# Sums in one piece, and the attention's first tiles beside the feed-forward's last steps, in a two-layer macaron block

## The chip, the core and the metric

The kernel runs on one core of a Trainium2 chip. It is written engine by engine: TensorE (PE) multiplies matrices and writes to PSUM, VectorE (DVE) and ScalarE (ACT) work on SBUF and PSUM, GpSimd (POOL) on SBUF, and SyncE (SP) issues transfers. Each engine takes its own instructions in order, and semaphores tie them together. The metric is the device time of one execution in microseconds; what counts is the median of several runs.

## The reference

One sequence of 2048 positions with 256 features passes two macaron layers. Every sub-block normalises its input first (LayerNorm), and its result is added to the residual.

```python
x = x + 0.5 * ffn0(layernorm(x))      # f0: ternary weights, silu(gate) * up, rms norm, projection
x = x + attn0(layernorm(x))           # 16 heads of 16, ALiBi bias, causal softmax
x = x + 0.5 * ffn0(layernorm(x))      # f1
x = x + 0.5 * ffn1(layernorm(x))      # f2: silu(gate) * up, 2 of 4 kept by magnitude, projection
x = x + attn1(layernorm(x))           # biases, rotary embedding (RoPE), causal softmax
x = x + 0.5 * ffn1(layernorm(x))      # f3

# attention, per head
scores = q @ k.T / 4 (+ alibi) ; scores = where(j > i, -inf, scores)
y = softmax(scores) @ v ; out = concat(y) @ W_o
```

## The kernel before

**Layout.** Features lie on partitions, positions run along the free axis. The 2048 positions are four chunks of 512 (`c`, NCH = 4); x and its normalised copy are one tile per chunk (`xs`, `xns`).

**Order.** The engines' instruction order is the order in which the Python code records them (`manual_schedule` for PE, ACT, DVE and POOL); only SP's transfers are put in order by the framework. Work that is to lie beside other work is a generator: each `next()` records one more piece, up to its `yield`. Such generators are the quantiser of the ternary weights, LayerNorm (`pieces`, in `background`), `sparsify`, the tail of a feed-forward, and the attention's preparation.

**Feed-forward.** `feed_forwards` goes through chunks and, in each, through eight steps f. A step is one gate-and-up product (`pg_f`), SiLU on ACT, a product on DVE. Steps of f0 and f1 work on three-part bf16 splits (12 matmuls); those of f2 and f3 are fp32, and every fourth one starts `sparsify` (`ge_f`, `ct_f`, `h_f` on DVE and POOL). The projection of a chunk (`po_f`) and its update of x lie in the next chunk's steps; the last chunk's come after all steps. In f0 the row sums of squares `ss_f` (POOL) go to the product `pss_f` before the projection. After every step, `beside` may record something of the attention that follows.

**Attention.** `attention` is a generator with two parts. The first yield hands out `first()`, whose pieces `beside0` and `beside1` record one per feed-forward step; `attend()` records what is left of it and then the whole rest. `prep_qk(c, "k")` and `prep_qk(c, "q")` multiply a chunk by the weights (`pp_k`, `pp_q`), split the result into three bf16 parts (ACT, DVE, POOL: `p_k`, `p_q`) and have SP write them to DRAM in six transfers (`dk<-p_k`, `dq<-p_q`). In layer 1 the rotary step comes before: two SP transfers swap halves (`sw`), POOL and DVE multiply by cosines and sines, DVE adds; the tiles `dn` and `sw` have one buffer there, and the generator has five pieces instead of two. `prep_v` makes v with a column of ones (`va`). `load(n, kc)` reads the four heads of group n (16 groups, four per chunk) back from DRAM, stacked so that one matmul over 96 rows gives the score of a head to fp32 accuracy, and adds rows for biases and maxima.

**Slots.** The rest runs over slots: a slot is a group n and a block `kb` of 128 keys (4, 8, 12 or 16 slots per group). For each slot:

- `st_pair`: keys by queries, two heads at a time, into a PSUM pair (`pst`); two pairs exist.
- `exp_pair`: the exponential on ACT, 128x1024 (`pT`).
- `mx_unit`: a tile of queries by keys of a later group (`pq`, one of three single PSUM banks), reduced to row maxima on DVE (`mx`). `mx_end` joins a group's maxima and splits them (`neg`); one step later `mx_turn` turns them with four small matmuls (`ptm`), ACT copies them (`qx`) and three transfers put them into the rows 96 to 98 of the group's q, so that the exponential's argument has its maximum subtracted.
- `av_part`: the sums `pav` of four heads, each in its own 32 columns of the array, over one half of the queries (part 0, part 1). On the diagonal, after part 0, `divide` transposes the 128 finished columns on DVE (`yt`), takes reciprocals (`rd`) and POOL multiplies (`zt`). Later `turn_back` and `output` finish a chunk (`pwo`).

On the diagonal a slot covers 512, 384, 256, then 128 queries; part 1 exists only if more than 256 are covered. A table `maxima` says which tiles go into which slot; slot -1 stands for the seven tiles that are needed before slot 0 (four of group 0, three of group 1). 140 of the 160 slots have tiles, all but the last ones.

In a slot with tiles the sums stand in two places: behind the first pair of heads the second half of the unit two slots back, behind the second pair the first half of the previous unit. Without tiles both halves of the previous unit stand together:

```python
for hp in (1, 0):
    ps = st_pair(n, kb, hp)
    mx_next(units[0], (2 - 2 * hp, 3 - 2 * hp))
    pTs[hp] = exp_pair(n, kb, hp, ps)
    sums(i - 2 + (hp == 0), hp)
```

The tiles of q, k and of the maxima are allocated in pools `kv` and `at` that open when the feed-forward's pool has closed; chunk 1's k, q and v are prepared between the seven tiles of slot -1. `need` records the pieces of a preparation until it is done.

Of the kernel before, what the change touches and what calls it, by code (L numbers as in the profile page):

```python
# [26 lines left out]
G = 4  # L27
# [19 lines left out]
def macaron_kernel(ctx: ExitStack, tc: tile.TileContext, a, out):  # L47
# [37 lines left out]
        )  # L85


    ident = cpool.tile([P, P], F32, name="ident")
    make_identity(nc, ident)
    ident_b = cpool.tile([P, P], BF16, name="ident_b")  # L90
    nc.vector.tensor_copy(ident_b, ident)

    mask_qk = cpool.tile([P, P], BF16, name="mask_qk")
    mask_kq = cpool.tile([P, P], BF16, name="mask_kq")
# [395 lines left out]
    def attention(layer, following):  # L490
# [9 lines left out]
        with ExitStack() as st:  # L500
# [20 lines left out]
            def prep_qk(c, what):  # L521

                ready(c)
                if what == "k" and c > 0:
                    nc.gpsimd.memset(va[c], 1.0)
                at = 0 if what == "q" else DC
                name = f"{layer}_{what}{c}"
                dn = ka.tile([P, DC, CH], F32, tag="dn", bufs=2 - layer, name=f"dn{name}")
                pt = [
                    ka.tile([P, DC, CH], BF16, tag=f"part{j}", bufs=1, name=f"p{j}{name}")  # L530
                    for j in range(3)
                ]
                for i in range(DC):
                    pp = ps_one(f"pp{name}_{i}")
                    for dc in range(DC):
                        nc.tensor.matmul(  # L536
                            pp,
                            lhsT=wqkv[:, dc, (at + i) * P : (at + i + 1) * P],
                            rhs=xns[c][:, dc, :],
                            start=dc == 0,  # L540
                            stop=dc == DC - 1,
                        )
                    if layer == 0:
                        nc.scalar.copy(pt[0][:, i, :], pp)
                        nc.vector.tensor_tensor(dn[:, i, :], pp, pt[0][:, i, :], ALU.subtract)
                    else:
                        nc.scalar.activation(
                            dn[:, i, :], pp, AF.Identity, bias=b_qk[:, at + i : at + i + 1]
                        )
                    if i == 0:  # L550
                        yield
                if layer == 1:

                    sw = ka.tile([P, DC, CH], F32, tag="sw", bufs=1, name=f"sw_{what}{c}")
                    for o in range(2):
                        nc.sync.dma_start(
                            out=sw[o * 64 : o * 64 + 64, :, :],
                            in_=dn[64 - o * 64 : 128 - o * 64, :, :],
                        )
# [14 lines left out]
                    for i in range(DC):  # L574
                        nc.gpsimd.tensor_tensor(sw[:, i, :], sw[:, i, :], cs[:, 1, :], ALU.mult)
                    yield
                    nc.vector.tensor_tensor(dn, dn, sw, ALU.add)
                    nc.scalar.copy(pt[0], dn)
                    nc.vector.tensor_tensor(dn, dn, pt[0], ALU.subtract)
                nc.scalar.copy(pt[1], dn)  # L580
                nc.gpsimd.tensor_tensor(pt[2], dn, pt[1], ALU.subtract)
                for j in range(3):
                    for m, part in enumerate(Q_PARTS if what == "q" else K_PARTS):
                        if part == j:
                            nc.sync.dma_start(
                                out=parts[what, c][:, m, :, :].rearrange("i p t -> p i t"),
                                in_=pt[j],
                            )
                done.add((what, c))
                yield  # L590
# [24 lines left out]
                        done.add(("v", c))  # L615
                    yield

            def first():
                nc.gpsimd.memset(va[0], 1.0)
                yield  # L620
                for work in (prep_qk(0, "k"), prep_qk(0, "q"), prep_v(0)):
                    yield from work

            yield first()
            kv = st.enter_context(tc.tile_pool(name=f"kv{layer}", bufs=1))
            ap = st.enter_context(tc.tile_pool(name=f"at{layer}", bufs=2))
            va += [values(kv, c) for c in range(1, NCH)]
            acc = ps_acc(f"pav{layer}")
            zts = {}
            zs = {}  # L630


            qs = {}
            ks = {}

            def load(n, kc):
                c, g = divmod(n, G)

                def stack(to, what, of, extra):
                    nc.sync.dma_start(  # L640
                        out=to[0:RM],
                        in_=parts[what, of][g // 2]
                        .rearrange("m (d u) t -> (m d) u t", u=HB)[:, g % 2 * 4 : g % 2 * 4 + 4, :],
                    )
# [12 lines left out]


# [40 lines left out]
            def mx_turn(n):  # L699
# [3 lines left out]
                for t in range(T):  # L703
# [4 lines left out]
                        start=True,  # L708
                        stop=True,
                    )  # L710
                qx = ap.tile([12, CH], BF16, tag="qx", bufs=2, name=f"qx{layer}_{n}")
                nc.scalar.copy(qx, pt)
                for m in range(3):
                    nc.sync.dma_start(out=qs[n][RM + m : RM + m + 1, :, :], in_=qx[4 * m : 4 * m + 4, :])
                turned_max.add(n)


            def banks(name, apart):
# [161 lines left out]
            def need(*what):  # L880
                while what not in done:
                    assert preps, what
                    step()

            left = {}
            for units in maxima.values():
                for u in units:
# [17 lines left out]

            def load_to(slot):
                while uses and uses[0][1] <= slot:
                    load(*uses.popleft()[0])
# [30 lines left out]
            for i, (n, kb) in enumerate(slots):  # L939
# [72 lines left out]

    def begin(layer, following):
        att = attention(layer, following)
        begun[:] = att, next(att)

    def beside0(s, at, f):
        if not quants and not begun:
            raw_scope.close()
            begin(0, "f1")  # L1020
        if at == NCH - 1:
            next(begun[1], None)

    def beside1(s, at, f):
        if s == 1 and at == 0 and f == FC // 2:
            own.close()
            ffn0_scope.close()
            begin(1, "f3")
        if s == 1 and (at == NCH - 1 or at == NCH - 2 and f >= FC // 2):
            next(begun[1], None)  # L1030
# [134 lines left out]
```

## Time and profile before

| | us |
|---|---|
| median of three runs | 1954.04 (1952.93 to 1957.03) |
| profiled execution, its own time | 1957.69 |
| its span | 1955.7 |
| PE busy | 1761.4 |
| DVE busy | 1361.6 |
| ACT busy | 894.2 |
| POOL busy | 458.4 |
| mean granted PE clock | 0.96 |

The profile shows one execution. A row of a timeline gives start, duration, engine, line, operation, output and inputs with shapes, a count, and in brackets how long the engine was idle before and what ended that. Durations of matmuls include the pipeline's depth, so what one occupies is read from the difference of two starts. Attention of layer 0 runs from about 240 to 766 us, that of layer 1 from about 1175 to 1766 us; the feed-forward f0 ends at 231, f1 and f2 fill about 766 to 1169, f3 the rest.

### The profile page before, as it was taken

Reading aid. Unit: us, or ns where it says so; the run is one execution under the profiler, and the core shown is the slowest. Engines: PE = TensorE matmul, PEld = TensorE weight load, DVE = VectorE, ACT = ScalarE, POOL = GpSimd, SP = SyncE. Lnnn points to the kernel's source line nnn. Section 1 sums busy time; section 2 is a strip of 40 time slices with the busy share of each in tenths; the row PEclk is TensorE's granted clock in tenths of the full one; section 3 lists DMA queues with packets and bytes.
Section 4 is the critical chain, followed back from the end, with each engine's and each line's share of the span. In section 5 each row is a group of like instructions: output and inputs, shape, how many; then the busy total and the mean of one; then the engine's idle time right before and its main releaser. Section 6 shows DMA issues by size and latency. Waiting matters only on the chain. (4 is left out here: it accounts for less than half of the span.)

```text
span 1955.7 us, 26994 instructions
## 1 busy us (share of the span) xinstructions
PE 1761.4 (90%) x10684; PEld 726.5 (37%) x10684; DVE 1361.6 (70%) x2384; ACT 894.2 (46%) x1112; POOL 458.4 (23%) x418
## 2 busy tenths in 40 slices
PE   5699789999999999789999876898999999998997
PEld 1233344433433333333444333433333333333443
DVE  7866377787788883666575655868877888825664
ACT  4343254555555668334422312445555656673220
POOL 3455321101000000455453432211111000003422
PEclk9799899999999999989999986999999999999999
DMA  4000252213211000200000115222122110000000
GB/s 129 1 1 33 82 148 83 73 54 102 62 45 46 28 28 2 73 1 0 1 11 0 54 61 158 82 73 92 52 69 86 43 43 26 18 1 0 11 11 22
DMA packets 50510, 93.10 MB, mean 48 GB/s; under 512 B 5424, under 2 KB 33072, under 8 KB 50128
## 3 DMA queue, kind: packets, MB, share of 16 engines
q1 hardware_dynamic: 49296, 89.28, 14.8%
q10 hardware_dynamic: 1088, 2.10, 0.3%
q8 instruction: 84, 1.38, 0.3%
q14 instruction: 42, 0.34, 0.1%
HBM read 59.51 MB, written 27.26 MB: 44 GB/s over the span
## 5 line engine op out<-in xcount | busy, mean ns | idle before, releaser
L682 DVE TENSOR_REDUCE mx<-pq 128x1 f32<-128x512 f32 (+3 forms) x1280 | 708.6, 603 | 158.5 <-PE pq L679 91.2
L753 ACT ACTIVATE pT<-pst 128x1024 f32<-128x1024 f32 (+3 forms) x614 | 542.6, 896 | 334.9 <-PE pst L733 196.8
L671 PE MATMUL pq<-k,q 105*128 105x512 bf16 (+7 forms) x1280 | 378.8, 353 | 74.7 <-DVE mx L682 52.3
L733 PE MATMUL pst<-q,k 99*128 99x512 bf16 (+7 forms) x1280 | 357.7, 354 | 5.1 <-ACT pT L753 4.2
L768 PE MATMUL pav<-pT,va 128*32 128x256 f32 (+1 forms) x4608 | 352.4, 382 | 5.2 <-DVE yt L789 5.0
L281 PE MATMUL pg_f<-xn,wgu 128*128 128x512 f32 x512 | 229.8, 602 | 11.5 <-DVE hr_f L318 11.5
L794 POOL TENSOR_TENSOR zt<-yt,rd 128x64 f32<-128x64 f32 x128 | 38.4, 300 | 795.2 <-DVE rd L793 795.1
L733 PEld LDWEIGHTS <-k 105*128 105x128 bf16 (+1 forms) x1280 | 101.5, 98 | 254.1 <-issue 218.4
L317 ACT ACTIVATE sl_f<-pg_f 128x512 f32<-128x512 f32 x128 | 76.0, 594 | 251.8 <-PE pg_f L281 175.0
L671 PEld LDWEIGHTS <-q 105*128 105x128 bf16 (+1 forms) x1280 | 124.5, 100 | 148.0 <-issue 44.3
L306 PE MATMUL pg_f<-xn,wgu 128*128 128x512 bf16 x512 | 156.2, 413 | 19.5 <-DVE wgu L170 6.8
L768 PEld LDWEIGHTS pav<-pT,va 128*32 128x32 f32 x4608 | 93.8, 108 | 208.7 <-issue 174.8
L281 PEld LDWEIGHTS pg_f<-xn,wgu 128*128 128x128 f32 x512 | 98.6, 193 | 136.9 <-issue 121.0
L306 PEld LDWEIGHTS <-wgu 128*128 128x128 bf16 x768 | 77.7, 101 | 166.9 <-issue 74.7
L292 PE MATMUL po_f<-h_f,wd 128*128 128x512 f32 x256 | 116.3, 608 | 17.3 <-DVE h_f L418 17.3
L340 POOL TENSOR_TENSOR ss_f<-ss_f,sq_f 128x512 f32<-128x512 f32 x56 | 91.1, 1628 | 111.5 <-ACT sq_f L339 111.3
L679 PE MATMUL pq<-mask_qk,ident_b 128*128 128x128 bf16 x512 | 107.3, 227 | 0.0
L741 PE MATMUL pst<-mask_kq,ident_b 128*128 128x128 bf16 x512 | 103.1, 222 | 0.0
L306 PE MATMUL pg_f<-xm_f,wgu 128*128 128x512 bf16 x256 | 85.3, 416 | 14.0 <-DVE xm_f L238 14.0
L318 DVE TENSOR_TENSOR h_f<-sl_f,pg_f 128x512 f32<-128x512 f32 x64 | 43.6, 682 | 76.4 <-ACT sl_f L317 76.3
L789 DVE STREAM_TRANSPOSE yt<-pav 128x128 f32<-128x128 f32 x128 | 39.8, 311 | 76.7 <-PE pav L768 76.7
L394 DVE TENSOR_TENSOR ge_f<-h_f 128x1536 bf16<-128x1536 f32 (+2 forms) x48 | 67.6, 1437 | 28.0 <-ACT h_f L387 28.0
(132 smaller groups left out, 1802.5 us busy)
## 6 DMA issues: line engine op xcount, KB each, us to landing
k<-dk SPq DMA_DIRECT2D x80, 384.0 KB
dk<-p_k SPq DMA_DIRECT2D x48, 256.0 KB
dq<-p_q SPq DMA_DIRECT2D x48, 256.0 KB
q<-dq SPq DMA_DIRECT2D x32, 384.0 KB
x<-in_xT ACTq DMA_DIRECT2D x4, 512.0 KB
raw<-in_w_gu SPq DMA_DIRECT2D x8, 256.0 KB
wgu<-in_w_gu SPq DMA_DIRECT2D x1, 2048.0 KB
cs_k<-in_cos_sin SPq DMA_DIRECT2D x4, 512.0 KB
```

What stands on the lines that cost most here:

```text
L281: nc.tensor.matmul(pg[:, half, :], lhsT=wgu[:, dc, half * F + f * P : half * F + (f + 1) * P], rhs=xn[:, dc, :], start=dc == 0, stop=dc == ...
L292: nc.tensor.matmul(po, lhsT=w[:, f, dc * P : (dc + 1) * P], rhs=h[:, f, :], start=f == 0, stop=f == FC - 1,)
L306: nc.tensor.matmul(pg[:, half, :], lhsT=wgu0[:, dc, half * F + f * P : half * F + (f + 1) * P], rhs=xp[part][:, dc, :], start=part == 0 an ...
L317: nc.scalar.activation(sl, pg[:, 0, :], AF.Silu)
L340: nc.gpsimd.tensor_tensor(ss, ss, sq, ALU.add)
L671: nc.tensor.matmul(pq, lhsT=qs[n][0:rows, hh, t * P : (t + 1) * P], rhs=ks[n, kc][0:rows, hh, 0:w], start=True, stop=kc < c,)
L679: nc.tensor.matmul(pq[:, w - P : w], lhsT=ident_b, rhs=mask_qk, start=False, stop=True)
L682: nc.vector.tensor_reduce(mxs[n][:, t, hh, kc : kc + 1], pq, AX.X, ALU.max)
L733: nc.tensor.matmul(ps[i][:, lo:CH], lhsT=ks[n, kc][0:rows, hh, t * P : (t + 1) * P], rhs=qs[n][0:rows, hh, lo:CH], start=True, stop=kc < c,)
L741: nc.tensor.matmul(ps[i][:, lo : lo + P], lhsT=ident_b, rhs=mask_kq, start=False, stop=True)
L753: nc.scalar.activation(pT[:, :, lo:CH], pair[:, :, lo:CH], AF.Exp, scale=0.25)
L768: nc.tensor.matmul(acc[hh * SLOT : (hh + 1) * SLOT, a:b], lhsT=va[kc][:, t, v0 : v0 + SLOT], rhs=pTs[hh // 2][:, hh % 2, a:b], start=kb == ...
```

## The change

1. In a slot with tiles both halves of the previous unit's sums are recorded together, behind the four heads' scores and tiles.
2. `first()` goes on: it loads groups 0 and 1, computes the seven tiles of slot -1 in half units of two heads, `mx_end` and `mx_turn` of group 0, and then begins k and q of chunk 1. It is advanced twice per feed-forward step, from the second half of the last chunk but one. `attend()` advances it until the seven tiles are done; what is left goes before v of chunk 1 into the slots.
3. For that, q and diagonal k of groups 0 and 1 of each four, the maxima, `neg` and `qx` move to the pool `ka`, which is open beside the feed-forward; the rings of four become two rings of two; `mx` has three buffers, `neg` and `qx` one.
4. The three transfers of a group's maxima are issued by ACT instead of SP.
5. The ones in `va` of chunks 1 to 3 are set together where the attention's pools open; the identity is made in bf16 directly.

```diff
-    ident = cpool.tile([P, P], F32, name="ident")
-    make_identity(nc, ident)
     ident_b = cpool.tile([P, P], BF16, name="ident_b")
-    nc.vector.tensor_copy(ident_b, ident)
+    make_identity(nc, ident_b)
...
-                if what == "k" and c > 0:
-                    nc.gpsimd.memset(va[c], 1.0)
...
+            pools = [ka]
+            def ring(n, other=False):
+                return pools[0 if other or n % 4 > 1 else -1]
...
-                need("k", kc)
-                ks[n, kc] = kv.tile(
-                    [P, 4, CH], BF16, tag="kd" if kc == c else "ko", bufs=4 if kc == c else 5,
+                ks[n, kc] = ring(n, kc < c).tile(
+                    [P, 4, CH], BF16, tag="kd" if kc == c else "ko", bufs=2 if kc == c else 5,
...
-                    need("q", c)
-                    qs[n] = kv.tile([P, 4, CH], BF16, tag="q", bufs=4, name=f"q{layer}_{n}")
+                    qs[n] = ring(n).tile([P, 4, CH], BF16, tag="q", bufs=2, name=f"q{layer}_{n}")
...
-                    mxs[n] = ap.tile([P, T, 4, NCH], F32, tag="mx", bufs=4, name=f"mx{layer}_{n}")
+                    mxs[n] = ka.tile([P, T, 4, NCH], F32, tag="mx", bufs=3, name=f"mx{layer}_{n}")
...
-                ng = ap.tile([P, T, 3, 4], F32, tag="neg", name=f"neg{layer}_{n}")
+                ng = ka.tile([P, T, 3, 4], F32, tag="neg", bufs=1, name=f"neg{layer}_{n}")
...
-                qx = ap.tile([12, CH], BF16, tag="qx", bufs=2, name=f"qx{layer}_{n}")
+                qx = ka.tile([12, CH], BF16, tag="qx", bufs=1, name=f"qx{layer}_{n}")
                 nc.scalar.copy(qx, pt)
                 for m in range(3):
-                    nc.sync.dma_start(out=qs[n][RM + m : RM + m + 1, :, :], in_=qx[4 * m : 4 * m + 4, :])
+                    nc.scalar.dma_start(out=qs[n][RM + m : RM + m + 1, :, :], in_=qx[4 * m : 4 * m + 4, :])
...
             def first():
                 nc.gpsimd.memset(va[0], 1.0)
                 yield
-                for work in (prep_qk(0, "k"), prep_qk(0, "q"), prep_v(0)):
+                for work in (prep_qk(0, "k"), prep_qk(0, "q")):
                     yield from work
+                load(0, 0)
+                yield from prep_v(0)
+                load(1, 0)
+                for n, t in FIRST:
+                    for heads in ((0, 1), (2, 3)):
+                        mx_unit(n, t, 0, heads)
+                        yield
+                    if (n, t) == (0, T - 1):
+                        mx_end(0)
+                        yield
+                        mx_turn(0)
+                        yield
+                done.add("maxima")
+                for work in (prep_qk(1, "k"), prep_qk(1, "q")):
+                    yield from work
+            FIRST = [(0, t) for t in range(T)] + [(1, t) for t in (2, 1, 0)]
...
+            pools.insert(0, kv)
             va += [values(kv, c) for c in range(1, NCH)]
+            for c in range(1, NCH):
+                nc.gpsimd.memset(va[c], 1.0)
...
-            load_to(-1)
-            preps.extend((prep_qk(1, "k"), prep_qk(1, "q"), prep_v(1)))
-            for unit in maxima[-1]:
-                mx_next(unit, (0, 1, 2, 3))
-                step()
-                now[0] += 1
-                run_due()
+            preps.extend((beginning, prep_v(1)))
...
                         pTs[hp] = exp_pair(n, kb, hp, ps)
-                        sums(i - 2 + (hp == 0), hp)
                 else:
...
                         pTs[hp] = exp_pair(n, kb, hp, ps)
-                    sums(i - 1, 1)
+
+                sums(i - 1, 1)
...
+    def go_on(s, at, f):
+        if at == NCH - 1 or at == NCH - 2 and f >= FC // 2:
+            for _ in range(2):
+                next(begun[1], None)
...
     def attend():
-        att, first = begun
-        for _ in first:
-            pass
+        att, first, done = begun
+        while "maxima" not in done:
+            next(first)
         next(att, None)
```

`load_to` in the slots now calls `need("k", kc)` and `need("q", n // G)` itself and skips what is loaded; `beside0` and `beside1` call `go_on`.

More of the change, by code (lines that the diff above doesn't have):

```diff
@@ L616, in prep_v @@
                     yield
-            def first():
-                nc.gpsimd.memset(va[0], 1.0)
-                yield
-                for work in (prep_qk(0, "k"), prep_qk(0, "q"), prep_v(0)):
[L622 to L630, printed above, removed]
+            pools = [ka]
             qs = {}
             ks = {}
+            def ring(n, other=False):
+                return pools[0 if other or n % 4 > 1 else -1]
             def load(n, kc):
@@ L710, in mx_turn, with first @@
                     )
-                qx = ap.tile([12, CH], BF16, tag="qx", bufs=2, name=f"qx{layer}_{n}")
+                qx = ka.tile([12, CH], BF16, tag="qx", bufs=1, name=f"qx{layer}_{n}")
                 nc.scalar.copy(qx, pt)
                 for m in range(3):
-                    nc.sync.dma_start(out=qs[n][RM + m : RM + m + 1, :, :], in_=qx[4 * m : 4 * m + 4, :])
+                    nc.scalar.dma_start(out=qs[n][RM + m : RM + m + 1, :, :], in_=qx[4 * m : 4 * m + 4, :])
                 turned_max.add(n)
+            def first():
+                nc.gpsimd.memset(va[0], 1.0)
+                yield
[12 more added lines that the diff above has]
+                        mx_turn(0)
+                        yield
+                done.add("maxima")
+                for work in (prep_qk(1, "k"), prep_qk(1, "q")):
+                    yield from work
+            FIRST = [(0, t) for t in range(T)] + [(1, t) for t in (2, 1, 0)]
+            beginning = first()
+            yield beginning, done
+            kv = st.enter_context(tc.tile_pool(name=f"kv{layer}", bufs=1))
+            ap = st.enter_context(tc.tile_pool(name=f"at{layer}", bufs=2))
+            pools.insert(0, kv)
+            va += [values(kv, c) for c in range(1, NCH)]
+            for c in range(1, NCH):
+                nc.gpsimd.memset(va[c], 1.0)
+            acc = ps_acc(f"pav{layer}")
+            zts = {}
+            zs = {}
             def banks(name, apart):
@@ L883, in need @@
                     step()
+            assert sorted(maxima.pop(-1)) == sorted((n, t, 0) for n, t in FIRST)
             left = {}
@@ L907, in load_to @@
                 while uses and uses[0][1] <= slot:
-                    load(*uses.popleft()[0])
-            load_to(-1)
-            preps.extend((prep_qk(1, "k"), prep_qk(1, "q"), prep_v(1)))
-            for unit in maxima[-1]:
-                mx_next(unit, (0, 1, 2, 3))
-                step()
-                now[0] += 1
-                run_due()
+                    (n, kc), _ = uses.popleft()
+                    if (n, kc) not in ks:
+                        need("k", kc)
+                        need("q", n // G)
+                        load(n, kc)
+            preps.extend((beginning, prep_v(1)))
             unsummed = deque()
@@ L1014, in begin @@
         att = attention(layer, following)
-        begun[:] = att, next(att)
+        begun[:] = att, *next(att)
+    def go_on(s, at, f):
+        if at == NCH - 1 or at == NCH - 2 and f >= FC // 2:
+            for _ in range(2):
+                next(begun[1], None)
     def beside0(s, at, f):
@@ L1020, in beside0 @@
             begin(0, "f1")
-        if at == NCH - 1:
-            next(begun[1], None)
+        go_on(s, at, f)
     def beside1(s, at, f):
@@ L1028, in beside1 @@
             begin(1, "f3")
-        if s == 1 and (at == NCH - 1 or at == NCH - 2 and f >= FC // 2):
-            next(begun[1], None)
+        if s == 1:
+            go_on(s, at, f)
     def attend():
-        att, first = begun
-        for _ in first:
-            pass
+        att, first, done = begun
+        while "maxima" not in done:
+            next(first)
         next(att, None)
```

## The prediction

> **What bounds the kernel now.** I read the page first (busy shares, slices), then the timelines of PE, VectorE (DVE) and SP inside an attention and where a feed-forward hands over to it, and last the instruction order of both kernels as built (no times in it).
>
> ```profile
> span 1955.7 us, 26994 instructions
> PE 1761.4 (90%) x10684; PEld 726.5 (37%) x10684; DVE 1361.6 (70%) x2384; ACT 894.2 (46%) x1112; POOL 458.4 (23%) x418
> PE   5699789999999999789999876898999999998997
> ...
> PEclk9799899999999999989999986999999999999999
> ```
>
> TensorE is the bound; slices 4 and 22 to 25 (near 220 us and 1150 to 1210 us) are the thin ones: a feed-forward ends there and attention begins.
>
> ```profile
> 645.57 0.64 PE L768 MATMUL pav<-pT,va 128*32 128x256 f32 x8
> 646.14 0.60 PE L733 MATMUL pst<-q,k 105*128 105x512 bf16 x2
> 646.58 0.59 PE L671 MATMUL pq<-k,q 105*128 105x512 bf16 x2
> 647.11 0.64 PE L768 MATMUL pav<-pT,va 128*32 128x256 f32 x8
> ...
> 767.19 1.07 PE L768 MATMUL pav<-pT,va 128*32 128x256 f32 x16
> 768.20 1.04 PE L733 MATMUL pst<-q,k 105*128 105x512 bf16 x4
> 769.16 1.07 PE L768 MATMUL pav<-pT,va 128*32 128x256 f32 x16
> ...
> 783.22 0.64 PE L768 MATMUL pav<-pT,va 128*32 128x256 f32 x8
> 784.37 0.64 PE L768 MATMUL pav<-pT,va 128*32 128x256 f32 x8 [0.51 <-DVE yt L789]
> ```
>
> Inside attention, differences of start times say what each piece takes: scores 0.44, tiles for the maxima 0.53, half of the sums 0.57, so 1.54 us per half slot and 3.08 per slot, without idle. Where the sums already run in one piece (groups 14 and 15, no maxima left) both halves take 1.01, not 1.14. The last row shows the price: between the halves of a diagonal unit stands `divide`, whose transpose `yt` reads the bank that the second half writes, and PE waits.
>
> ```profile
> 240.25 0.27 PE L671 MATMUL pq<-k,q 105*128 105x128 bf16 x1 [8.71 <-DMA q<-in_q_rows]
> ...
> 1160.02 9.16 PE L292 MATMUL po_f<-h_f,wd 128*128 128x512 f32 x16 [10.26 <-DVE h_f L418]
> ...
> 1175.32 0.26 PE L671 MATMUL pq<-k,q 99*128 99x128 bf16 x1 [4.42 <-DMA q<-in_q_rows]
> ...
> 1216.64 0.48 PE L671 MATMUL pq<-k,q 99*128 99x384 bf16 x1 [8.15 <-DVE mx L682]
> ```
>
> The hand-over of layer 0 waits 8.71 us for the first k and q; layer 1 waits for sparsify, for q, and then 8.15 behind chunk 1's preparation on DVE.
>
> ```profile
> 201.71 4.99 SPq L585 DMA_DIRECT2D dq<-p_q  x6
> ...
> 1143.75 4.91 SPq L585 DMA_DIRECT2D dq<-p_q  x6
> ...
> L714 SPq DMA_DIRECT2D q<-qx x96: 572/578/695, 263.7 to 1727.6; - x96
> ```
>
> SP writes q to DRAM and reads it back; and it issues 96 rows of maxima at 0.58 us each.
>
> **The change, part by part** (plus is time gained).
>
> *Sums in one piece.* A slot becomes 4 x 0.44 + 0.09 + 1.01 = 2.86 us, 0.22 less for each pair of halves that now runs together: 84 full units (36, 32, 16 in chunks 3, 2, 1) and 28 diagonal ones (the first two of groups 0 to 13) per layer, 224 in all, 49 us. Against it, the slot's fourth tile needs the buffer of its first, whose reduction (start 0.42 after the matmul, 0.65 long, 0.06 to PE) ends 0.05 late: 168 x 0.05 = 8. And in each diagonal pair (56 in all) PE now waits for `yt`, which stands on DVE behind the slot's four reductions; before, a score and a maxima block lay between and hid it. In chunk 3's second diagonal slot DVE comes in 0.9 late (from the 512-wide slot before and `mx_end`, 0.6), four 384-wide reductions of 0.505 end at 2.9, `yt` at 3.2, PE goes on at 3.3; the first half ended at 2.35: 0.95. The third slot (256 wide): reductions end at 2.16, PE goes on at 2.55 after 1.85: 0.7. Floor: the 0.51 above, with DVE empty; ceiling: about 1. I take 0.78, so 44. Sum 49 - 8 - 44 = -3, bounds +13 to -15.
>
> *Rows of maxima on ACT.* The three transfers wait for the copy `qx` ahead of them, so ACT stands still for 3 x 0.58 = 1.7 us (ACT's own four issues, of x, are 0.45 to 0.48 each), and the next exponentials are behind them. In a full slot the exponential (1.02) then starts 1.9 late against a slack of 0.8, and PE finds its score buffer held for 0.8 to 0.9. That is groups 6, 7, 10 and 11, 8 x 0.9 = 7; the other 24 fall in narrow diagonal slots, 1 together. -8, bounds -2 to -15. The Trainium skill (DMA: Bandwidth & Descriptors, "Issuing engines are not separate DMA queues") says that another issuing engine only saves the sequencer's time, usually small beside the transfer. By that this part is 0 and my sum 2 slower instead of 10; I keep the row's 0.58, since an in-order ACT pays it. SP gets 56 us back, but PE waited for q<-qx only 2.3 us in all.
>
> *Layer 0's hand-over.* Two steps of `first` go beside each feed-forward step from chunk 2's second half: k, q, v of chunk 0 move from chunk 3 to chunk 2 (6 x 1.72 = 10.3 us of PE), the seven tiles of groups 0 and 1 come in (5.7 us with turning), and chunk 1 gets only its first k product in, not q. New is a wait: `pq` of tile 0 stands in PE's queue before chunk 3's first gate, 6.2 us (v 1.72, gate 2.7, v 1.72) behind q's last product. Before, that product ended at 200.85 and SP issued the last write at 206.7, 5.85 later. The write and the read back are shown by nothing just alike: rows with several transfers under way give 3.4 (layer 1's `sw_q`, issued by 1205.57, used at 1208.95) and 5.2 (q<-dq at 1230.05, used at 1235.3), 8.6; the skill's fit (same page, "Anatomy of one DMA", for the GpSimd path) of 2.0 us plus bytes over 436 GB/s gives 2.6 + 2.9 = 5.5. I take 7, since the load shares with one other only: 5.85 + 7 - 6.2 = 6.7 us idle, and 2 for the clock (219 to 222 us: 0.63 per matmul, later 0.39, after 3.96 idle). By the page's fit it is 5.2. All of the feed-forward's products are queued behind it on PE; behind the load on SP stand q of group 1 and loads into memory that the feed-forward still holds, none due before its end, and nothing on POOL.
> Chunk 3's first step then ends at 168.4 + 10.3 + 6.7 + 2 - 2.9 (the waits for split at 165 are covered) + 0.2 = 184.7. Steps 1 to 7: 44.3 - 10.3 + 5.5 = 39.5 by PE; DVE has 29 + 12 = 41 there, so 42.5. Then 4.5 to `pss` (covering the k product) and 14.3 of projection: first scores at 246, before 267. The first four slots took 17.3; with 8.6 of chunk 1's k, q, v that ran ahead of them, 26: slot 4 at 272, before 284.3. +12, bounds +4 to +18.
>
> *Layer 1's hand-over.* Rope makes `prep_qk` five steps, so the 24 end inside group 1. q's last steps hang on `f_3_1`; in the old place its last write was issued at 1148.66, 11.1 after the gate step it hung on. With 7 for the round trip and 7.75 of PE work (v, gate 3.43, norm, v) ahead of `pq`, PE stands 10.3, and 2.3 for the clock (9.16 against 6.87 above), in a stretch with PE 100% busy. Added before the projection's end: tiles 3.9, v 1.7, two reductions ahead of sparsify 1.0. So it ends 19 later. The 10.26 stays. Then ten reductions, slot 0, and, because group 4's load at slot 1 needs chunk 1's k and q, the whole preparation in one piece: with one `dn` and one `sw` buffer, each half is 11.6 (SP 1.2, landing 3.4, POOL 3.5, add 1.2, copy 1.05, subtract 1.23), and between them 5 (copy, POOL 2.1, two evictions). pp_k at +10.3, DVE free at +39; before 1216.1, which is +47. Slot 1's maxima are queued behind that. 19 - 8 = -11, bounds -16 to 0.
>
> *The rest costs nothing:* `ident_b` without its copy lies under the first load; three memsets of 1.05 on POOL at once are done before POOL's next operand (over 5 us away); two-buffer rings of q and k turn over after the same four groups; single `qx`, `neg` and three `mx` are freed several slots before reuse.
>
> **Sum:** -3 - 8 + 12 - 11 = -10: 1957.7 + 10 = 1967.7 for the profiled execution. That one lies 3.7 above the median of the runs, so 1964.0.
>
> **Rivals.**
> 1. *The turns of the array decide: faster.* Every merge pays 0.22 at 224 places, and PE's wait for `yt` is near its floor. For it: the rows at 767 and 784. Against: DVE is about 90% busy in a full slot, so `yt` isn't first in line. With the other parts at -7, it is faster by over 4 us from a mean wait under (41 - 7 - 4) / 56 = 0.54. At 0.5, with round trips of 5.5 us and ACT at -3: 41 - 28 - 3 + 13.5 - 9.5 = +14, so 1940.
> 2. *The queues bind harder.* DVE limits chunk 3's steps by 5 us more (it is over 90% full there), ACT loses 15, the round trip is 8.6 in layer 1 (2 more, and 1 of clock), the wait is 1.0: 41 - 56 - 15 + 7 - 14 = -37, so 1991.
> 3. *Parts cancel:* wait 0.65, ACT -5: 41 - 36 - 5 + 12 - 11 = +1, so 1953. That chunk 1's q and k do not get beside the feed-forward, as the words of the change say, is in all of these.
>
> **How the numbers follow.** Forecast (1958 to 1978) 0.50, rival 1 0.28, rival 2 0.10, rival 3 0.12. A measurement of this kernel tells about 0.2%, 4 us, from nothing: faster 0.28, same 0.12, slower 0.60. Signs are mixed, so the range takes in most of both sides: 1942 to 1984; the forecast alone is 1958 to 1978.
>
> **What would show it.** `pq` of tile 0 waiting for q<-dq 5 to 8 us (layer 0) and 9 to 12 (layer 1); `pav` idle on `yt` near 40 us in all (12.6 with weight loads now); full slots of 2.9 us; a hole of 1.7 us on ACT behind each `qx`; layer 0's first scores near 246. I am wrong if `pq` starts without a wait, or if `pav` waits under 0.5 each.

## The result, and the profile after

| | before | after |
|---|---|---|
| median of the runs, us | 1953.75 | 2017.43 |
| profiled execution: span, us | 1955.7 | 2014.3 |

The changed kernel is slower: the ratio is 1.0318, 95% interval 1.0304 to 1.0331, some 62 us. The prediction had 10 us, and the result lies outside its range. The profile of the changed kernel has this span, these busy shares, and these slices (counted from 0) of PE and of the granted clock:

```profile
span 2014.3 us, 26939 instructions
...
PE 1736.0 (86%) x10684; PEld 760.4 (38%) x10684; DVE 1343.7 (67%) x2383; ACT 880.6 (44%) x1112; POOL 456.4 (23%) x418
...
PE   4697878889999999799999484888888999998997
...
PEclk9899999999999999999999797898998999999999
```

PE does the same 10684 matmuls in 25 us less busy time, and yet the span is 59 longer: PE waits about 84 us more. The thin slices are where they were, but wider: 3 to 8, where layer 0's feed-forward hands over and attention begins, and 22 to 30 for layer 1.

A slot of group 12 without a diagonal, on PE's timeline (start, duration, engine, line, operation, count, and in brackets the idle time before it and what ended it):

```profile
660.15 0.60 PE L753 MATMUL pst<-q,k 105*128 105x512 bf16 x2
...
662.06 1.07 PE L788 MATMUL pav<-pT,va 128*32 128x256 f32 x16
663.06 0.60 PE L753 MATMUL pst<-q,k 105*128 105x512 bf16 x2
```

From one slot's scores to the next it takes 2.91 us where it took 3.08; the sums run in one piece of 1.00. That part of the change does what it says. At the hand-overs, one row of the kernel before (the last norm product `pss` of layer 0's feed-forward), then rows of the changed kernel:

```profile
217.23 2.08 PE L353 MATMUL pss_f<-ss_f,ones_m 128*128 128x512 f32 x2 [3.96 <-POOL ss_f L340]
```

```profile
181.75 0.27 PE L656 MATMUL pq<-k,q 105*128 105x128 bf16 x1 [8.46 <-issue]
...
198.08 0.32 PE L656 MATMUL pq<-k,q 105*128 105x384 bf16 x1 [4.39 <-DVE tt_rms_f L204]
...
246.89 1.12 PE L351 MATMUL pss_f<-ss_f,ones_m 128*128 128x512 f32 x2 [1.73 <-POOL ss_f L338]
...
1146.34 0.29 PE L656 MATMUL pq<-k,q 99*128 99x128 bf16 x1 [18.91 <-DMA q<-dq]
...
1159.43 0.37 PE L656 MATMUL pq<-k,q 99*128 99x256 bf16 x1 [6.42 <-DVE mx L667]
...
1247.66 0.48 PE L656 MATMUL pq<-k,q 99*128 99x384 bf16 x1 [12.39 <-ACT dn_q L543]
...
1260.38 0.48 PE L656 MATMUL pq<-k,q 99*128 99x384 bf16 x1 [10.86 <-DVE mx L667]
```

In layer 0 the first tile of the attention stands 8.5 us in front of chunk 3's gates; the third tile waits 4.4 for a bank that a transpose of the feed-forward (`tt_rms_f`) still has to read; `pss` comes at 246.9, where before it came at 217.2. In layer 1 the first tile waits 18.9 for q, the second 6.4 for reductions on DVE, and slots 0 and 1 wait 23 more for chunk 1's preparation and the reductions behind it. For layer 0's first tile the profile names no releaser (`issue`). The next rows show it: SP issues the load of q at 177.9, when PE has been ready for 4.6 us. They are SP's writes of q to DRAM, the load of layer 0, and the rows of maxima in ACT's queue:

```profile
170.87 5.17 SPq L581 DMA_DIRECT2D dq<-p_q  x6
177.91 0.79 SPq L627 DMA_DIRECT2D q<-dq  x2
...
1135.87 4.90 SPq L581 DMA_DIRECT2D dq<-p_q  x6
...
L699 ACTq DMA_DIRECT2D q<-qx x96: 580/580/1187, 224.2 to 1784.2; - x96
```

Where the time goes over the run can be read at the copy `qx`, which ACT makes once for each of the 16 groups of a layer. The table has the start of that copy before, and how much later it came in other kernels (us, one profiled execution each; e1 to e9 are the experiments below):

```
layer group before  after  e1     e2     e3     e4     e7     e9
0     1      275.7  +5.0   +1.4   +0.7   +2.2   -1.1   -7.8  -18.1
0     4      315.8  +13.0  +3.5   +2.3   +6.6   -0.9   -4.6  -13.6
0     9      485.5  +22.6  +8.2   +8.6   +4.9   -4.7   -6.3  -15.2
0     15     753.2  +18.8  +2.2   +10.0  +3.7   -20.0  -6.3  -16.4
1     1     1221.0  +45.3  +4.4   +13.2  +26.2  -18.5  -8.6  -13.1
1     4     1270.2  +49.0  +5.8   +13.7  +22.8  -19.4  -14.1 -16.5
1     9     1446.5  +56.5  +9.9   +13.6  +23.4  -22.6  -16.5 -15.9
1     15    1725.7  +56.6  +6.2   +22.0  +22.3  -34.5  -16.5 -17.0
```

Layer 0 loses 13 by group 4 and 10 more by group 9, then gains 4 back; layer 1's hand-over adds 26, and its groups 1 to 9 another 11.

### The profile page after: what moved, and what is told of

It is laid out like the page before. It is cut to its first block, busy times and chain, and to the rows that moved or that the text cites. A ratio compares the mean times of both kernels' runs of the same rounds, so it can differ in the third digit from the quotient of the medians.

```text
span 2014.3 us, 26939 instructions
## 1 busy us (share of the span) xinstructions
PE 1736.0 (86%) x10684; PEld 760.4 (38%) x10684; DVE 1343.7 (67%) x2383; ACT 880.6 (44%) x1112; POOL 456.4 (23%) x418
## 5 line engine op out<-in xcount | busy, mean ns | idle before, releaser
L667 DVE TENSOR_REDUCE mx<-pq 128x1 f32<-128x512 f32 (+3 forms) x1280 | 693.1, 602 | 165.2 <-PE pq L664 99.7
L773 ACT ACTIVATE pT<-pst 128x1024 f32<-128x1024 f32 (+3 forms) x614 | 528.5, 897 | 329.4 <-PE pst L753 185.2
L656 PE MATMUL pq<-k,q 105*128 105x512 bf16 (+7 forms) x1280 | 390.4, 352 | 134.2 <-DVE mx L667 71.3
L788 PE MATMUL pav<-pT,va 128*32 128x256 f32 (+1 forms) x4608 | 321.3, 381 | 34.2 <-DVE yt L809 34.0
L788 PEld LDWEIGHTS pav<-pT,va 128*32 128x32 f32 x4608 | 111.6, 109 | 236.2 <-issue 125.0
L753 PEld LDWEIGHTS <-k 105*128 105x128 bf16 (+1 forms) x1280 | 112.9, 99 | 196.6 <-issue 130.4
L290 PE MATMUL po_f<-h_f,wd 128*128 128x512 f32 x256 | 116.1, 607 | 12.3 <-DVE h_f L416 12.3
L316 DVE TENSOR_TENSOR hr_f<-sl_f,pg_f 128x512 f32<-128x512 f32 x64 | 43.7, 683 | 66.9 <-ACT sl_f L315 66.9
## 6 DMA issues: line engine op xcount, KB each, us to landing
dk<-p_k SPq DMA_DIRECT2D x48, 256.0 KB
dq<-p_q SPq DMA_DIRECT2D x48, 256.0 KB
raw<-in_w_gu SPq DMA_DIRECT2D x8, 256.0 KB
```

Of the source, the lines that this page charges most:

```text
L290: nc.tensor.matmul(po, lhsT=w[:, f, dc * P : (dc + 1) * P], rhs=h[:, f, :], start=f == 0, stop=f == FC - 1,)
L316: nc.vector.tensor_tensor(to, sl, pg[:, 1, :], ALU.mult)
L656: nc.tensor.matmul(pq, lhsT=qs[n][0:rows, hh, t * P : (t + 1) * P], rhs=ks[n, kc][0:rows, hh, 0:w], start=True, stop=kc < c,)
L667: nc.vector.tensor_reduce(mxs[n][:, t, hh, kc : kc + 1], pq, AX.X, ALU.max)
L753: nc.tensor.matmul(ps[i][:, lo:CH], lhsT=ks[n, kc][0:rows, hh, t * P : (t + 1) * P], rhs=qs[n][0:rows, hh, lo:CH], start=True, stop=kc < c,)
L773: nc.scalar.activation(pT[:, :, lo:CH], pair[:, :, lo:CH], AF.Exp, scale=0.25)
```

## The experiments

**The change, one part at a time (e1 to e3).** e1 is the kernel before with this edit alone:

```diff
                         pTs[hp] = exp_pair(n, kb, hp, ps)
-                        sums(i - 2 + (hp == 0), hp)
                 else:
...
-                    sums(i - 1, 1)
+
+                sums(i - 1, 1)
```

> The kernel before with both halves of the sums in one piece in every slot, and nothing else of the change. Theory (the loss is made at the two hand-overs and in the chunks 0 and 1 behind them, the sums are as predicted): 3 us slower, between 10 faster and 10 slower; PE waits about 0.5 us for yt in each of some 56 diagonal slots, and a slot with maxima and without a diagonal takes 2.9 us. Rival (the loss in chunks 0 and 1 comes from the sums standing behind a late exponential): 20 to 30 us slower, with the loss in groups 0 to 7.

Measured: 1962.4, ratio 1.0039 [1.0026, 1.0052], 8 us slower, inside the theory's bounds. In the table it loses 8 us up to group 9 of layer 0 and takes 6 back by group 15, where many slots have no diagonal. So the rival is wrong in size, and right that the early groups pay.

e2 is the kernel before with `nc.sync` turned into `nc.scalar` at the three transfers of `mx_turn`:

> The kernel before with the three transfers of the rows of maxima issued by ACT in place of SP, and nothing else. Theory (as predicted): 8 us slower, 2 to 15; a hole of 1.7 to 1.9 us on ACT behind each qx. First rival (an issue on another engine only saves SP's time): within 2 us of the kernel before. Second rival (ACT is the bound of the narrow slots in chunks 0 and 1, so every one of 32 holes is paid in full): 32 x 1.2 = 38 us slower.

Measured: 1975.8, ratio 1.0118 [1.0097, 1.0138], 23 us slower: between the theory and the second rival, three times what was predicted. The table shows it growing along layer 0, by some 8 us from group 4 to group 15. The same place in a narrow diagonal slot of group 12, on ACT's timeline of the kernel before and then in e2 (there with the PE row that follows):

```profile
657.75 0.57 ACT L712 CAST qx<-ptm 12x512 bf16<-12x512 f32 x1 [0.35 <-PE ptm L704]
658.24 0.58 ACT L753 ACTIVATE pT<-pst 128x512 f32<-128x512 f32 x1
```

```profile
666.51 0.57 ACT L712 CAST qx<-ptm 12x512 bf16<-12x512 f32 x1 [0.35 <-PE ptm L704]
667.11 1.82 ACTq L714 DMA_DIRECT2D q<-qx  x3
668.98 1.08 ACT L753 ACTIVATE pT<-pst 128x512 f32<-128x512 f32 x2 [1.90 <-DMA q<-qx]
669.63 0.22 PE L733 MATMUL pst<-q,k 105*128 105x128 bf16 x1 [0.56 <-ACT pT L753]
```

Before, the exponential follows the copy by 0.5 us; in e2 it starts 2.5 after it, and PE's next score waits 0.56 for the score buffer. The slot is narrow, its exponential only 0.58 long, and still PE pays.

e3 is the changed kernel with the sums in halves and the transfers on SP again, so that the early tiles and the smaller rings remain:

> The changed kernel with the sums in halves as before and the rows of maxima on SP as before: what remains is the attention's early tiles, the early maxima and the preparation of chunk 1, with the smaller rings. Theory (the hand-overs carry the loss): 45 us slower, 35 to 60; first scores of layer 0 near 258, as in the changed kernel, groups 0 to 7 slower than before by about 25 in the two layers together. Rival (the hand-over is worth about what was predicted, and the loss comes from sums and ACT together): at most 10 us slower, groups 2 to 7 as fast as before.

Measured: 1981.8, ratio 1.0146 [1.0127, 1.0165], 29 us slower by the ratio (23.6 by the two profiled spans), with the first scores of layer 0 at 256.0: less than the theory, more than the rival. The table puts some 4 us of it into layer 0 and the rest into layer 1. What the three ratios have above one adds up to 0.0303, and the whole has 0.0318: within the intervals the three parts account for all of it, and the sizes that were wrong are those of ACT and of the hand-over.

**Sums: what takes their gain (e4).** e1 with the division behind both halves:

```diff
-                if part == 0 and kc == c:
+                if part == 1 and kc == c:
                     divide(n, t)
```

> The kernel before with the sums in one piece, and the division of a diagonal unit recorded behind both halves of its sums and not between them, so that PE has nothing to wait for between the halves. Theory (the wait for yt takes nearly all that the merges bring): 30 to 40 us faster than before. Rival (the merges bring little by themselves, since DVE or ACT then sets the pace of a slot): within 8 us of the kernel with only the sums in one piece.

Measured: 1922.1, ratio 0.9834 [0.9821, 0.9848], 32 us faster than before and 40 faster than e1. Two rows of the waits (engine, instruction and what it waited for: us in total, times, longest), of e1 and of e4:

```profile
PE pav L768 <- DVE yt L789: 34.6, 66, 0.7
```

```profile
PE pav L768 <- DVE yt L789: 1.2, 2, 0.6
```

The wait is gone, and what is left is the merges alone. By the profiled spans (before, e1 and e4: 1955.7, 1962.1, 1919.6) the merges bring 36 us and the wait for `yt` costs 42.5, 0.76 for each of the 56 diagonal units. The view's 34.6 us in 66 waits, 0.52 each, is lower, because it counts the modelled end of the first half as busy: by start times such halves are 1.22 us apart in e1 and merged halves 0.50 in e4 (256 wide), and 1.02 against 0.40 (192 wide), so 0.6 to 0.7 each.

**ACT: hole or transfer (e5, e6).** In e5 POOL issues all three transfers; in e6 ACT issues the middle one only:

```diff
-                    nc.sync.dma_start(out=qs[n][RM + m : RM + m + 1, :, :], in_=qx[4 * m : 4 * m + 4, :])
+                    (nc.sync, nc.scalar, nc.sync)[m].dma_start(out=qs[n][RM + m : RM + m + 1, :, :], in_=qx[4 * m : 4 * m + 4, :])
```

> The kernel before with the three transfers of the rows of maxima issued by POOL in place of SP. Theory (what ACT's issues cost is the hole on ACT itself, ahead of the exponentials queued behind it, not the transfer): within 3 us of the kernel before, since POOL is busy 4 to 8% inside attention. Rival (SP's place in the queue order matters, or the transfer becomes slower from another engine): 15 us slower or more, as with ACT.

> The kernel before with only one of the three transfers of the rows of maxima issued by ACT, the middle one, and two still by SP. Theory (PE pays for the part of ACT's hole that exceeds its slack, about 1.0 us in a slot: 1.8 with three issues gives 0.6 to 0.9 per group): a hole of 0.6 us is inside the slack, so within 3 us of the kernel before. Rival (each issue on ACT is paid, whatever its neighbours): a third of the 22 us that three issues cost, 7 us slower.

Measured: both 1.0006 of before ([0.9995, 1.0017] and [0.9995, 1.0018]), no difference that can be told. The transfer is as good from another engine, so the price in e2 is ACT's own time; and one issue of 0.58 us lies inside ACT's slack where three do not. PE's waits for exponentials, in the kernel before, in e2 and in e6:

```profile
PE pst L733 <- ACT pT L753: 4.2, 7, 0.9
```

```profile
PE pst L733 <- ACT pT L753: 20.7, 26, 2.5
```

```profile
PE pst L733 <- ACT pT L753: 5.7, 7, 1.3
```

The 16.5 us between the first two account for most of the 22.5 us by which e2's span is longer; where the rest lies was not followed up (ACT's square roots and copies of the preparation and of the norms stand behind some issues too). PE's timelines of the two kernels say which slots pay: 2.7 of the 16.5 us stand ahead of scores of 512 queries, and 13.8 ahead of narrower ones. A narrow one, the longest (0.9 before), and a full one, in e2:

```profile
294.63 0.27 PE L733 MATMUL pst<-q,k 105*128 105x256 bf16 x1 [2.52 <-ACT pT L753]
...
570.16 0.38 PE L733 MATMUL pst<-q,k 105*128 105x512 bf16 x1 [0.44 <-ACT pT L753]
```

**Hand-over: why the first tile waits so long in layer 1.** Rows of e3 from the timeline of all engines, ahead of that wait:

```profile
1109.98 1.48 POOL L407 TENSOR_TENSOR ct_f<-ct_f,ge_f 128x512 bf16<-128x512 bf16 x1
1111.42 2.84 POOL L571 TENSOR_TENSOR sw_q<-sw_q,cs_k 128x512 f32<-128x512 f32 x2
...
1114.73 1.21 DVE L573 TENSOR_TENSOR dn_q<-dn_q,sw_q 128x1024 f32<-128x1024 f32 x1
...
1117.10 4.90 SPq L581 DMA_DIRECT2D dq<-p_q  x6
...
1127.09 0.29 PE L656 MATMUL pq<-k,q 99*128 99x128 bf16 x1 [18.44 <-DMA q<-dq]
```

q's rotation `sw_q` stands on POOL behind four operations of sparsify (the last at 1109.98), its sum on DVE behind it and behind sparsify's operations there; the last of six writes is issued at 1122.0, and 5.1 later PE has q. PE was ready at 1108.65. Whether the place in the queue is the cause is tried by moving it.

**The place of the first tile (e7, e9).** e7 is e3 with chunk 1's k and q ahead of the tiles; e9 is e3 with empty steps ahead of them:

```diff
                 load(1, 0)
+                for work in (prep_qk(1, "k"), prep_qk(1, "q")):
+                    yield from work
                 for n, t in FIRST:
...
                 done.add("maxima")
-                for work in (prep_qk(1, "k"), prep_qk(1, "q")):
-                    yield from work
+                yield
```

```diff
                 load(1, 0)
+                for _ in range(4 + 4 * layer):
+                    yield
                 for n, t in FIRST:
```

> The kernel with only the hand-over part of the change, but with the order inside it turned round: chunk 0's k, q and v and then chunk 1's k and q go beside the feed-forward, and the seven tiles, which need k and q back from DRAM, come last, most of them behind the feed-forward. Theory (the early tiles cost, because PE's queue stands behind a load that isn't there and behind reductions on a late DVE, and because chunk 1's preparation is left in one piece for slots 0 and 1): 8 us faster than before, between 20 faster and equal; no wait of PE over 5 us for a q that comes back from DRAM. Rival (the smaller rings and the early loads carry the loss): 20 us slower or more, as with the tiles first.

> The kernel with only the hand-over part of the change, with empty steps between the loads of chunk 0's q and the first tile: four in layer 0 (two feed-forward steps, some 11 us) and eight in layer 1 (four steps, some 18 us). The order of everything else is the same: the tiles still come before chunk 1's k and q, whose preparation then falls wholly to the first slots. Theory (the wait for the round trip of q is the largest single loss in layer 1, and in layer 0 it is 8 of some 22, the rest being tiles that wait for a bank held by a late DVE): the waits of 8.4 and 18.4 us shrink to under 3, and the kernel is 12 us faster than with the tiles undelayed, 1969. Rival (the wait only moves: what PE doesn't lose at the tile it loses behind the feed-forward, at the tiles' reductions and at the preparation of chunk 1 in one piece): within 4 us of 1981.

Measured: e7 1942.1, ratio 0.9943 [0.9922, 0.9965]; e9 1944.7, ratio 0.9949 [0.9932, 0.9967]. Both are 10 to 11 us faster than before, so 37 to 40 faster than e3. For e9 the theory named the right cause and gave it a third of its size, and the rival is refuted. Both kernels keep the smaller rings, the early loads and item 5 of the change, so those don't carry the loss; that was e7's rival. PE's timeline of e9 at the first tile of layer 0 and at slots 0 and 1 of layer 1:

```profile
181.81 0.22 PE L656 MATMUL pq<-k,q 105*128 105x128 bf16 x1 [1.80 <-issue]
...
1190.91 0.48 PE L656 MATMUL pq<-k,q 99*128 99x384 bf16 x1 [12.42 <-ACT dn_q L543]
1203.60 0.48 PE L656 MATMUL pq<-k,q 99*128 99x384 bf16 x1 [10.82 <-DVE mx L667]
```

The wait for q is 1.8 us in layer 0 and gone in layer 1, where it was 18.4; layer 1 adds 19 us to the copies' lateness in e3 and nothing in e9 (group 15 in the table). Chunk 1's preparation still holds up slots 0 and 1 for 23 us, as in e3, so it isn't what separates the two kernels. How a wait of 8.4 us grew shows in the windows of layer 0 (stretch, its length, then busy time and instructions of PE, PEld, DVE, ACT and POOL, the granted clock, DMA), from the same start up to `pss` (in e9 1.4 us short of it), first e3 and then e9:

```profile
168.40:188.40 20.00, 9.95 (x37) 4.83 (x36) 8.71 (x13) 5.88 (x11) 7.13 (x4) 0.74 0.44 137
188.40:244.20 55.80, 43.65 (x193) 19.07 (x192) 30.28 (x60) 16.38 (x23) 18.96 (x14) 0.91 0.00 1
```

```profile
168.40:188.40 20.00, 17.05 (x75) 7.99 (x74) 13.41 (x20) 12.88 (x19) 11.98 (x8) 1.00 0.50 157
188.40:225.00 36.60, 28.04 (x140) 12.94 (x141) 22.52 (x42) 8.62 (x14) 13.36 (x10) 1.00 0.00 1
```

In e3 PE is half idle in the first 20 us, and the clock is 0.74 there and 0.91 in the next 56; in e9 it is 1.00 throughout. `pss` comes at 244.2 in e3 and at 226.4 in e9. Of these 17.8 us, 9.8 are waits (in e3 22.1 us of idle time ahead of products up to and with `pss`: 8.36, 1.73, 4.39, 0.34, 2.65, 2.73 and 1.92; in e9 12.3). The rest is the clock, and work that e9 has moved behind `pss`; the two were not separated.

e7 has a wait of its own. Chunk 1's product stands in PE's queue before chunk 1's norm is ready:

```profile
1117.71 2.93 PE L532 MATMUL pp_k<-xn,wqkv 128*128 128x512 f32 x3 [17.68 <-POOL xn L267]
```

It loses 17.7 us here, and e9 loses its 23 in slots 0 and 1 instead.

**Together (e8, e10, e11, e12).** e8 is the kernel before with e4's sums and e7's hand-over; e10 has the sums of e1 and the transfers of e2; e11 is the whole change with e9's empty steps.

> The sums in one piece with the division behind both halves, the rows of maxima on SP, and the hand-over with the tiles last. Theory (the parts add up): 32 + 8 = 40 us faster than before, 1914. Rival (with the sums faster, DVE is late at the hand-over and the second gain is lost): 1922, as with the sums alone.

> The kernel before with the sums in one piece and the rows of maxima issued by ACT, without the hand-over part. Theory (the three parts are independent, and the 6 us by which the whole change is worse than their sum lie at the hand-over): 8 + 22 = 30 us slower than before, 1984. Rival (the two share the slack: with shorter slots the hole on ACT is paid more often): 36 us slower, 1990.

> The whole change (sums in one piece, rows of maxima on ACT, early tiles) with the empty steps of the delayed tiles, four in layer 0 and eight in layer 1, and nothing else different. Theory (the place of the first tile in PE's queue is worth 37 us by itself, whatever the sums and ACT do): 2017 - 37 = 1980, still 25 slower than before, for what sums and ACT cost. Rival (the 6 us by which the whole is worse than its parts lie in that wait too): 1983 - 11 = 1972.

Measured: e8 1909.6, ratio 0.9761 [0.9742, 0.9780], 44 us faster by the medians and 47 by the ratio: the gains, 32 and 11, add up. e10 1983.0, ratio 1.0146 [1.0126, 1.0167]: the theory holds, sums and ACT don't share a loss. e11 1979.3, ratio 1.0113 [1.0094, 1.0131]: some 40 of the change's 62 us go with the empty steps alone, as the theory had it. What stays, 22, lies between e10's 29 and the 19 that e10 and e9 make together. The rival's 1972 lies just below the interval, which starts at 1973; the six runs spread from 1971 to 1981, so it is not far off.

e12 takes e4's sums, SP for the rows, e9's empty steps, and spreads chunk 1's preparation in layer 1 (`first_tiles` is the loop over the tiles, cut out of `first`):

```diff
+                tiles = first_tiles()
+                chunk1 = chain(prep_qk(1, "k"), prep_qk(1, "q"))
+                for _ in tiles:
+                    yield
+                    if layer == 1:
+                        next(chunk1, None)
+                        yield
```

> A version put together from the runs: the sums in one piece with the division behind both halves, the rows of maxima on SP, the tiles delayed as before, and in layer 1 chunk 1's k and q recorded step by step between the tiles in place of behind them all. Theory (the gains of 32 and 11 add up, and of the 23 us that PE waits in layer 1's slots 0 and 1 for chunk 1's preparation about 12 go): 55 us faster than before, 1899. Rival (the preparation's evictions delay the tiles' reductions on DVE by as much as they bring the preparation forward): 43 us faster, 1911.

Measured: 1903.2, ratio 0.9731 [0.9717, 0.9745], 52 us faster than before, between the two and nearer the theory. Slot 1's wait in layer 1 is still there, and shorter:

```profile
1172.74 0.48 PE L657 MATMUL pq<-k,q 99*128 99x384 bf16 x1 [8.95 <-DVE mx L668]
```

## Why the prediction was right or wrong

The direction was right and the size wrong, 62 us against 10. By its own terms, in profiled spans (us, plus is time gained):

| step | predicted | measured | by |
|---|---|---|---|
| sums in one piece | -3 | -6 | e1 |
| of it: merges, after the fourth tile's delay | +41 | +36 | e4 |
| of it: PE's wait for `yt` | -44 | -42.5 | e1 less e4 |
| rows of maxima on ACT | -8 | -22.5 | e2 |
| hand-over of layer 0 | +12 | -4 | e3, table |
| hand-over of layer 1 | -11 | -19 to -22 | e3, table |
| whole | -10 | -59 | after |

The measured parts add up to 51 to 55, not 59. They are single executions; the ratios, which take all runs, leave 3 of the 62 us open, within their intervals.

*Sums: right.* Gain and price were each met within 5 us. The merge's 0.22, worked out from blocks that already ran in one piece, fits a full slot that is 0.17 shorter, since 0.05 was taken off for the fourth tile; and so does 0.78 for a diagonal unit (0.76 by the spans). The waits view of the changed kernel has 34.0 us in 66 waits of `pav` for `yt`, where the prediction named 40. Rival 1 asked for a mean wait under 0.54. By the view's 0.52 that limit is just met; by what the wait costs, which is what the rival's sum needs, it is not.

*ACT: mis-sized.* The hole was right (1.8 to 1.9 us), and so was the choice of the trace over the page "DMA: Bandwidth & Descriptors" of the Trainium skill ("Issuing engines are not separate DMA queues"): its rule gives nothing for the transfer, and e5 agrees, but e2 costs 23 us because exponentials that PE needs stand behind the issues on ACT. The term that failed is "the other 24 fall in narrow diagonal slots, 1 together". A narrow exponential is shorter, but so is the slot: e2's timeline has 13.8 us of PE's new waits ahead of scores of fewer than 512 queries, where the prediction had 1, and 2.7 ahead of full ones, where it had 7. Some 6 of the 22.5 us are not located.

*Layer 0: four terms too small.* The wait of tile 0 was foreseen as 6.7 and was 8.5: the last write was issued 3 us later than assumed, at 176.0, while the round trip was shorter, 5.7 from that issue to PE's start, not 7. The page's fit for the GpSimd path ("Anatomy of one DMA"), which gave 5.5, was nearer than the 7 I preferred. The clock, taken as 2 us, was 0.74 and then 0.91 over 76 us of e3; busy time times the share that is missing gives an estimate of 6.5 us. The 42.5 for "Steps 1 to 7", set by DVE, left out that the tiles take their turn in the three single banks of the feed-forward's own norms: PE waited 1.7, 4.4, 2.7 and 2.7 us (in e3) for banks that a late DVE still had to read. First scores came at 258.7 in the changed kernel (256.0 in e3), not at 246. And the first four slots, with chunk 1's preparation in them, took 33.0 in e3 (256.0 to 289.0) instead of 26, with one wait of 6.4 for that preparation:

```profile
271.95 0.48 PE L656 MATMUL pq<-k,q 105*128 105x384 bf16 x1 [6.42 <-DVE dn_q L541]
```

*Layer 1: the wait was 18.9, not 10.3.* The round trip was again short, 5.6. What failed was to carry over from the old place "11.1 after the gate step it hung on" for the last write: in the new place sparsify stands on POOL and DVE between the rotation's pieces, and the last write came 13.3 after PE was ready for the tile, where the sum had 3.3. A second term was put at nothing: the tiles behind the first wait too, 6.4, 2.3 and 3.0 us in e3, for banks that DVE's reductions still have to read. And "The 10.26 stays" was wrong the other way: that wait for sparsify shrank to 5.3. In all the down-projection starts 34.4 later in e3 than before, of which layer 0 had left 3.7, so 31 against the 19 of the prediction. The gain in chunk 1's preparation, 8, was right: from the down-projection's start behind its wait to slot 1's tile it took 56.6 before (1160.02 to 1216.64) and 48.5 in e3:

```profile
1194.41 9.50 PE L290 MATMUL po_f<-h_f,wd 128*128 128x512 f32 x16 [5.33 <-DVE h_f L416]
...
1242.90 0.48 PE L656 MATMUL pq<-k,q 99*128 99x384 bf16 x1 [10.90 <-DVE mx L667]
```

*Rival 2* had the right direction, and rightly more loss on ACT and in layer 0, but two fifths of the whole missing; its wait of 1.0 in the sums and its round trip of 8.6 were both too long.

## What to carry over

An instruction that is moved ahead of other work on an in-order queue must be placed by when its data is there, not by where its engine has room: here four to eight empty steps turned a loss of 29 us into a gain of 10. Give a transfer's issue to the engine with slack where it stands, and count the slack in the shortest slot. When a fusion brings nothing, look for the wait inside it: moving one division behind the fused block was worth 40 us.

## What was not expected of the hardware

- Where PE had stood idle the clock was lower too: with PE half idle over 20 us (9.95 busy), the granted clock was 0.74, and 0.91 over the next 56; in the kernel whose first tile waited 1.8 and not 8.4 us it was 1.00 over both stretches. This is one execution of each.
- POOL issued the same transfers in 0.52 us each, against 0.58 on ACT and on SP, and with POOL issuing them the kernel was as fast as before.
- From the last of six write issues to DRAM until PE could use the block read back took 5.1 to 5.7 us, in both layers.
